# A convolution and a Laplace layer on one Trainium2 core: sums for two places in one run of matmuls, and three tiles for the mixed rows

## Chip, cores and metric

The kernel runs on one core of a Trainium2 chip. The metric is the device time of one execution in microseconds (us); the time before is the median of three runs.

## The reference

The input x has 16 images of 16 channels, 256 by 256, in float32. Two layers follow each other. Each normalises its input over groups of two channels and adds its result to that input.

```python
x = x + _L0_conv_ref(_gn(x), L0_conv_weight)          # a 3x3 circular convolution
x = x + _L1_conv_ref(_gn(x), ty, tx, pole1, pole2, residue)
```

The second layer is where the change lies:

```python
alpha = fft2(x)                                        # b i o x
A  = 1 / (omega1[:, None, None, None] - weights_pole1[None])
Bm = 1 / (omega2[:, None, None, None] - weights_pole2[None])
S  = einsum('ikpq,oikp,xikq->oxik', weights_residue, A, Bm)
output_residue1 = einsum('biox,oxik->bkox', alpha, S)  # mixing of channels, one matrix per frequency
x1 = ifft2(output_residue1).real
...
F  = einsum('kbpq,bipz->kbiqz', output_residue2, E1)
x2 = einsum('kbiqz,biqx->kizx', F, E2).real            # transient, with E1 = exp(pole1 ty), E2 = exp(pole2 tx)
return x1 + x2 / Nx / Ny
```

## The kernel before, in words

The work goes in four stages.

1. Convolution (to about 596 us): for each image, 3x3 convolution by small matmuls (L305). Results go to DRAM tensors `vD`. Tables for the second layer are made beside it.
2. Transform (to about 1190 us): channel by channel, folds on VectorE (DVE) and GpSimd (POOL), matmuls along y (L777, L785) and along x (L820). The spectra go to the DRAM tensor `aD`.
3. Mixing (to about 1866 us): for every frequency the 16 input channels are combined into 16 output channels. Spectra are read from `aD`, mixed rows are written to `yD`. This is the stage of the change.
4. Inverse transform, transient and output (to the end), L1325 to L1399.

**The mixing stage.** It runs over 32 groups g of four frequency rows, with four places n in each (L1222 to L1242). The instructions stand in each engine's queue in the order in which the loop writes them. At a place the loop does this:

- `sums(n, w_now)` (L1025): 16 matmuls, 32 on the hardware, on 64x32 tiles of the array, for the matrices S of the *next* group. They fill two PSUM banks; the pool of these banks, `p_s`, has four.
- `spread` (L1043): copies the two banks into the tile `sg` of the next group. For each bank, ScalarE (ACT) makes one copy (L1049) and DVE one shuffle (L1052).
- `mix` four times (L1111): 8 matmuls each, 16 on the hardware, of `sg` with the spectra `abd`, on 128x64 tiles, into a bank of the pool `p_mix`, which has four.
- Four copies from these banks into a tile `yt` (L1233): the first three on ACT and the last on DVE, or two and two when ACT has exponentials to do (`late`). The pool of `yt` has two buffers.
- Four stores of `yt` to `yD` (`store`, L1134), 128 KB each, and loads of the next group's spectra `abd` (`load`): at place 1 four of 256 KB (L1102), two before and two after the stores; at places 2 and 3 four of 128 KB each after the stores (L1107). The tiles `abd` have one buffer each, so a load follows the mixing that reads it. All of these are issued by SyncE (SP), in order.
- One step of `weights(g + 2)` on DVE (L903 to L919), at the third place the weight tile `w` on POOL (L930), and one step of `make_exps` (L1161 to L1214), which makes the tables of E1 and E2 on POOL and ACT.

Before the loop, `first_sums` (L1054) makes the first group's matrices and `finish_projections` (L1085) multiplies with the constant `jmat`. In the last group there are no sums; the first frequency is corrected by `unmix_first` (L1139), which loads four pieces from `yD` and stores them again.

Pools lie in SBUF one above the other. A tile that takes the memory of an earlier one waits for the last user of that one.

Of the kernel before, what the change touches and what calls it, by code (L numbers as in the profile page):

```python
# [9 lines left out]
FP = mybir.dt.float32  # L10
AF = mybir.ActivationFunctionType
ALU = mybir.AluOpType
# [4 lines left out]
B = 16  # L17
C = 16
N = 256
P = 128  # L20
PI = float(np.pi)
# [3 lines left out]
def conv_then_laplace_kernel(ctx: ExitStack, tc: tile.TileContext, a: dict, out: bass.AP):  # L25
# [15 lines left out]
    nc = tc.nc  # L41
    x = a["x"]

    cp = ctx.enter_context(tc.tile_pool(name="const", bufs=1))
# [6 lines left out]

    later_loads = []

    def const(name, shape):
        t = cp.tile(shape, FP, name=name, tag=name)
        later_loads.append((t, a[name]))
        return t

    cols = const("cols", [P, 24])
    kmask = const("kmask", [P, C])  # L60
    fold2 = const("fold2", [P, 2, 64])
    o2 = cp.tile([P, B, 2, 16], FP, name="o2", tag="o2")
    proj = cp.tile([P, 2, B, 16, 2], FP, name="proj", tag="proj")
    jmat = cp.tile([P, 3, P], FP, name="jmat", tag="jmat")

    def pitched(name, rows, row, *split):

# [27 lines left out]

    ptab = ExitStack()
    tp = ptab.enter_context(tc.tile_pool(name="tables", bufs=1))
    vmr = tp.tile([P, 2, B, C], FP, name="vmr", tag="vmr")


# [54 lines left out]
    own = m16[:, 0:C:2]  # L155
    load_consts()
    halves[1] = [load_x(1, h) for h in range(2)]
    nc.sync.dma_start(out=jmat, in_=a["jmat"])
    ones = tp.tile([P, P], FP, name="ones", tag="ones")
    nc.vector.memset(ones, 1.0)  # L160
    tiny = wp.tile([P, 8], FP, name="tiny", tag="tiny")
# [524 lines left out]
    for g in range(24 * B + 3):  # L686
# [4 lines left out]
        b, n = divmod(g, 24)  # L691
# [27 lines left out]
    def pool(stage, name, bufs=1, **kw):  # L719
        return stage.enter_context(tc.tile_pool(name=name, bufs=bufs, reuse_waits="tile", **kw))  # L720
# [11 lines left out]
    u0 = pool(p1, "u0")  # L732
# [162 lines left out]
    def weights(g):  # L895

        shape = [P, 32, 4]
        u = up["u" if g else "u0"].tile([P, 4, 32, 4], FP, name="u", tag="u")  # L900
        w, den, e, f = (u[:, j] for j in range(4))
        pr2, pre, pim = (prU[:, j].unsqueeze(2).to_broadcast(shape) for j in range(3))
        nc.vector.tensor_tensor(  # L903
            w,
            omg[:, g].unsqueeze(1).to_broadcast(shape),
            pims.unsqueeze(2).to_broadcast(shape),
            ALU.subtract,
        )
        nc.vector.tensor_tensor(den, w, w, ALU.mult)
        nc.vector.tensor_tensor(den, den, pr2, ALU.add)  # L910
        yield
        nc.vector.reciprocal(den, den)

        nc.vector.scalar_tensor_tensor(e, w, m1, pre, ALU.mult, ALU.add)
        nc.vector.scalar_tensor_tensor(f, w, nm0, pim, ALU.mult, ALU.add)
        yield
        v = up["v"].tile([P, 32, 2, 4], FP, name="v", tag="v")
        nc.vector.tensor_tensor(v[:, :, 0], e, den, ALU.mult)
        nc.vector.tensor_tensor(v[:, :, 1], f, den, ALU.mult)  # L919
        if g == 0:  # L920
            yield
        wt = wp.tile([P, 4, 8, 32], FP, name="w", tag="w")
        v2 = v.rearrange("p a r s -> p a (r s)")
        w4 = wt.rearrange("p a k (i m) -> p (a k) i m", i=4)
        if g == 0:
            for i in range(4):
                nc.scalar.activation(w4[:, :, i], v2, AF.Copy, scale=m4[:, i : i + 1])
            return wt
        full = [P, 32, 4, 8]
        nc.gpsimd.tensor_tensor(  # L930
            w4,
            v2.unsqueeze(2).to_broadcast(full),
            m4.unsqueeze(1).unsqueeze(3).to_broadcast(full),
            ALU.mult,
        )
        return wt
# [44 lines left out]
    ptab.close()  # L981


    yp = pool(p2, "yt", 2)
    g0 = pool(p2, "sg0")
    a0 = pool(p2, "abd0")
    wp = pool(p2, "w", 2)
    ep = pool(p2, "exps")
    up["u"] = pool(p2, "u")
    a1 = pool(p2, "abd2")  # L990
    zp = pool(p2, "between")
    tp = pool(p2, "ct")
    a2 = pool(p2, "abd3")
    g1 = pool(p2, "sg1")
# [10 lines left out]
        z.tile([P, 4, 4, 16, B], FP, name=f"abd{j}", tag=f"abd{j}") for j, z in ((2, a1), (3, a2))  # L1005
    ]

    zp.tile([P, 384], FP, name="between", tag="between")
    ct = tp.tile([P, 4, 8, N], FP, name="ct", tag="ct")
    nc.sync.dma_start(out=ct, in_=cD)  # L1010
    def next_step(steps, w):
# [42 lines left out]
    def first_sums():  # L1054
# [27 lines left out]
            load(0, jq)  # L1082
        return sg, w1

    def finish_projections():  # L1085


        for ro in range(2):
            ps = pm.tile([P, B, 16], FP, name="ps_o", tag="ps_mix")
            nc.tensor.matmul(ps, lhsT=jmat[:, 0], rhs=accs[:, ro], start=True, stop=False)  # L1090
            nc.tensor.matmul(ps, lhsT=jmat[:, 2 - ro], rhs=accs[:, 1 - ro], start=False, stop=True)
            nc.vector.tensor_copy(o2[:, :, ro], ps)

    def load(g, jq, rows=range(4)):

# [65 lines left out]
    def make_exps(which):  # L1161


        pl = ep.tile([P, C, 2], FP, name="s_pl", tag="s_pl")
        nc.sync.dma_start(out=pl, in_=a[f"pole_e{which + 1}"])
        t = ep.tile([P, N], FP, name="s_t", tag="s_t")
        nc.sync.dma_start(out=t, in_=a[("ty", "tx")[which]].to_broadcast([P, N]))
        sign, phase, turns = (cols[:, 2 + 3 * which + j : 3 + 3 * which + j] for j in range(3))
        pim = ep.tile([P, C], FP, name="s_pim", tag="s_pim")
        for _ in range(4):  # L1170
            yield
        nc.gpsimd.tensor_scalar(pim, pl[:, :, 1], sign, None, ALU.mult)
        for q in range(8):
            th = ep.tile([P, 2, N], FP, name="s_th", tag="s_th")
            rn = ep.tile([P, 2, N], FP, name="s_rn", tag="s_rn")
            tmp = ep.tile([P, 2, N], FP, name="s_tmp", tag="s_tmp")
            ex = ep.tile([P, 2, N], FP, name="s_ex", tag="s_ex")
            for j in range(2):
                i = 2 * q + j
                nc.gpsimd.tensor_scalar(th[:, j], t, pim[:, i : i + 1], None, ALU.mult)  # L1180
            nc.gpsimd.tensor_scalar(rn, th, 1.0 / (2 * PI), turns, ALU.mult, ALU.add)
            magic = 1.5 * 2.0**23
            nc.gpsimd.tensor_scalar(rn, rn, magic, None, ALU.add)
            nc.gpsimd.tensor_scalar(rn, rn, magic, None, ALU.subtract)
            yield
            c1 = 6.28125
            c2 = float(np.float32(1.93500518798828125e-3))
            c3 = 2 * np.pi - c1 - c2
            for c in (c1, c2, c3):
                nc.gpsimd.tensor_scalar(tmp, rn, float(c), None, ALU.mult)  # L1190
                nc.gpsimd.tensor_tensor(th, th, tmp, ALU.subtract)
                if c == c2:
                    yield
            nc.gpsimd.tensor_scalar(th, th, phase, 3.1415925, ALU.add, ALU.min)
            nc.gpsimd.tensor_scalar(th, th, -3.1415925, None, ALU.max)
            for j in range(2):
                i = 2 * q + j
                nc.scalar.activation(ex[:, j], t, AF.Exp, scale=pl[:, i, 0:1])
            yield True
            yield  # L1200
            nc.scalar.activation(th, th, AF.Sin)
            yield True
            nc.gpsimd.tensor_tensor(th, th, ex, ALU.mult)
            for op, eo in ((ALU.add, 0), (ALU.subtract, 1)):
                nc.gpsimd.tensor_tensor(
                    ex[:, :, eo * P : eo * P + P], th[:, :, 0:P], th[:, :, N - 1 : P - 1 : -1], op
                )
            yield
            for o in range(2 - which):
                nc.sync.dma_start(  # L1210
                    out=eD[which][o, :, 2 * q : 2 * q + 2].rearrange("p i e t -> p i (e t)"),
                    in_=ex,
                )
            yield  # L1214
# [1 line left out]
    p2.enter_context(tc.manual_schedule())  # L1216
    accs = yp.tile([P, 2, B, 16], FP, name="accs", tag="yt")
    ahead, wt = first_sums()
    finish_projections()
    unmix = None  # L1220
    exps, late = chain(make_exps(0), make_exps(1)), None
    for g in range(32):  # L1222
        sg, w_now = ahead, wt
        steps = weights(g + 2) if g < 30 else iter(())
        ahead = new_sg(g + 1) if g < 31 else None
        for n in range(4):
            evict = sums(n, w_now) if ahead is not None else []
            yt = yp.tile([P, 2, 4 * B, 16], FP, name="yt", tag="yt")
            if evict:
                spread(n, (ahead, [z.rearrange("p q n -> p n q") for z in evict]))  # L1230
            for m in range(4):
                o, src = mix(4 * n + m, sg, yt)
                (nc.vector.tensor_copy if m >= (2 if late else 3) else nc.scalar.copy)(o, src)  # L1233
            if n == 1 and g < 31:
                load(g + 1, n, (0, 1))
            store(g, n, yt)
            if g < 31:
                load(g + 1, n, (2, 3) if n == 1 else range(4))
            if n == 1 and unmix is not None:
                next(unmix, None)  # L1240
            wt = next_step(steps, None) or wt
            late = g and next(exps, None)  # L1242
        if g == 30:
            unmix = unmix_first()
            next(unmix)
# [364 lines left out]
```

## Time and profile before

| | |
|---|---|
| Median of three runs | 2617.32 us (2607.34 to 2626.05) |
| Profiled execution, its own time | 2623.94 us |
| Its span | 2622.1 us |
| PE busy, whole span | 2468.6 us (94%) |
| DVE / ACT / POOL busy | 1980.8 / 1432.6 / 1290.5 us |
| Granted TensorE clock | 0.986 |
| Mixing stage in the profile | about 1222 to 1866 us |
| Mixing matmuls (L1120), busy | 482.2 us, 8192 instructions |
| Copies into yt on ACT (L1233) | 184.1 us, 352 instructions of 592 ns |
| Idle time of ACT before these | 55.8 us, 42.2 of it until a store `yD<-yt` has landed |

Times are those of one profiled execution. "Busy" is the union of an engine's instructions; a wait is put down to the instruction or DMA that ended last before the waiting one began. PEld is the loading of weights into the array, which overlaps PE. SPq is SyncE's queue: all of its time is the issue of DMAs, and a wait for a semaphore is inside an instruction's duration.

### The profile page before, as it was taken

Reading aid. Unit: us, or ns where it says so; the run is one execution under the profiler, and the core shown is the slowest. Engines: PE = TensorE matmul, PEld = TensorE weight load, DVE = VectorE, ACT = ScalarE, POOL = GpSimd, SP = SyncE. Lnnn points to the kernel's source line nnn. Section 1 sums busy time; section 2 is a strip of 40 time slices with the busy share of each in tenths; the row PEclk is TensorE's granted clock in tenths of the full one; section 3 lists DMA queues with packets and bytes.
Section 4 is the critical chain, followed back from the end, with each engine's and each line's share of the span. In section 5 each row is a group of like instructions: output and inputs, shape, how many; then the busy total and the mean of one; then the engine's idle time right before and its main releaser. Section 6 shows DMA issues by size and latency. Waiting matters only on the chain.

```text
span 2622.1 us, 84262 instructions
## 1 busy us (share of the span) xinstructions
PE 2468.6 (94%) x35314; PEld 1885.3 (72%) x35314; DVE 1980.8 (76%) x3772; ACT 1432.6 (55%) x2599; POOL 1290.5 (49%) x1179
## 2 busy tenths in 40 slices
PE   5998999989999999998999999999799999999998
PEld 2444455567777777775878778788688888888887
DVE  7777788848888888887877878887276676667666
ACT  2565566666666666665666656666244444444443
POOL 1333378433333333333666645766555565555553
PEclk9999999989999999999999999999899999999999
DMA  7888878854655655655777777777988888888884
GB/s 274 276 279 282 294 270 294 297 211 177 240 195 209 242 220 194 245 225 190 225 229 214 226 225 222 222 227 228 253 302 289 291 292 279 299 289 287 291 287 174
DMA packets 318011, 653.17 MB, mean 249 GB/s; under 512 B 49174, under 2 KB 163990, under 8 KB 305728
## 3 DMA queue, kind: packets, MB, share of 16 engines
q1 hardware_dynamic: 316464, 640.57, 72.4%
q8 instruction: 278, 4.55, 0.7%
q0 software_dynamic: 896, 3.02, 0.4%
q10 hardware_dynamic: 272, 4.19, 0.4%
q14 instruction: 101, 0.83, 0.1%
HBM read 368.15 MB, written 280.36 MB: 247 GB/s over the span
## 4 chain that ended last, share of the span: by engine, by line
PE 58%; DVE 7%; DMA 4%; SPq 3%; ACT 3%; POOL 2%; issue 1%; ACTq 0%; DVEq 0%; POOLq 0%
PE ps_mix L1120 9%; PE ps_y L777 9%; PE ps_y L785 8%; PE ps_p L1361 7%; PE ps_f L1385 7%; PE ps_f L1386 7%; PE ps_x L820 5%; DMA yD<-yt 4%; PE ps_s L1032 2%; SPq L1134 2%; PE ps_h L1345 2%; PE psd L805 1%; DVE r L1394 1%; DVE ol L1396 1%; DVE ol L1397 1%
## 5 line engine op out<-in xcount | busy, mean ns | idle before, releaser
L1120 PE MATMUL ps_mix<-abd,sg 128*64 128x128 f32 x8192 | 482.2, 276 | 39.4 <-DMA yD<-yt 16.6
L1120 PEld LDWEIGHTS ps_mix<-abd,sg 128*64 128x64 f32 x8192 | 451.9, 138 | 92.9 <-ACT yt L1233 55.7
L1325 POOL TENSOR_TENSOR u<-yk 128x512 f32<-128x512 f32 (+1 forms) x268 | 358.2, 1369 | 314.7 <-PE ps_p L1361 249.1
L305 PE MATMUL ps_conv<-xt,wc 32*32 32x512 f32 x12288 | 445.6, 602 | 36.0 <-issue 26.1
L305 PEld LDWEIGHTS ps_conv<-xt,wc 32*32 32x32 f32 x12288 | 251.1, 103 | 217.6 <-issue 127.0
L793 ACT ACTIVATE t<-ps_y,vmr 128x384 f32<-128x384 f32 x512 | 297.1, 580 | 161.1 <-PE ps_y L785 161.1
L1052 DVE STREAM_SHUFFLE sg<-ps_s 128x512 f32<-128x512 f32 (+1 forms) x264 | 329.1, 1316 | 0.0
L777 PE MATMUL ps_y<-tabE,vq 128*128 128x256 f32 x1024 | 313.2, 388 | 11.0 <-DVE vq L766 9.4
L785 PE MATMUL ps_y<-tabO,vq 128*128 128x256 f32 x1024 | 305.9, 380 | 0.0
L275 POOL TENSOR_TENSOR pair<-pair,far 128x1024 f32<-128x1024 f32 x64 | 151.7, 2370 | 304.1 <-DVE pair L272 207.7
L1385 PE MATMUL ps_f<-pt,inv 128*128 128x256 f32 x1008 | 300.4, 380 | 0.0
L1386 PE MATMUL ps_f<-hs,ey 128*128 128x256 f32 x1008 | 299.8, 379 | 0.0
L1361 PEld LDWEIGHTS ps_p<-inv,u 128*128 128x128 f32 x2048 | 268.9, 193 | 35.4 <-POOL u L1329 10.9
L1389 DVE TENSOR_TENSOR r<-ps_f,q 128x256 f32<-128x256 f32 x256 | 107.0, 418 | 241.9 <-ACT q L1388 241.9
L1361 PE MATMUL ps_p<-inv,u 128*128 128x128 f32 x2048 | 276.2, 278 | 9.8 <-POOL u L1329 9.7
L1049 ACT ACTIVATE sg<-ps_s,mcol 128x512 f32<-128x512 f32 (+1 forms) x264 | 179.3, 689 | 192.2 <-DVE sg L1052 117.1
L777 PEld LDWEIGHTS ps_y<-tabE,vq 128*128 128x128 f32 x1024 | 189.6, 191 | 87.5 <-ACT q L833 51.2
L1388 ACT COPY q<-ps_f 128x256 f32<-128x256 f32 x256 | 95.4, 373 | 274.7 <-PE ps_f L1386 250.4
L1363 ACT COPY pt<-ps_p 128x512 f32<-128x512 f32 x256 | 151.5, 592 | 134.9 <-PE ps_p L1361 134.9
L765 POOL TENSOR_TENSOR vq<-vf 128x512 f32<-128x512 f32 x64 | 81.4, 1272 | 291.6 <-DVE vf L769 281.5
L785 PEld LDWEIGHTS ps_y<-tabO,vq 128*128 128x128 f32 x1024 | 195.4, 191 | 26.9
L1233 ACT COPY yt<-ps_mix 128x512 f32<-128x512 f32 x352 | 184.1, 592 | 55.8 <-DMA yD<-yt 42.2
(237 smaller groups left out, 3993.6 us busy)
## 6 DMA issues: line engine op xcount, KB each, us to landing
xt<-in_x SPq DMA_DIRECT2D x288, 258.0 KB
vD<-pair SPq DMA_DIRECT2D x256, 256.0 KB
yD<-yt SPq DMA_DIRECT2D x512, 128.0 KB
vl<-vD SPq DMA_DIRECT2D x128, 512.0 KB
out_y<-ol SPq DMA_DIRECT2D x128, 512.0 KB
s<-vD SPq DMA_DIRECT2D x126, 512.0 KB
aD<-spec SPq DMA_DIRECT2D x15, 4096.0 KB
yk<-yD SPq DMA_DIRECT2D x60, 1024.0 KB
```

The costliest lines, as they stand in the source:

```text
L305: nc.tensor.matmul(acc[r][32 * c : 32 * c + 32], lhsT=ready[b][0][rows, phase, tap], rhs=halves[b][u // 2][rows, q : q + 5 : 4, 2 - tap : ...
L777: nc.tensor.matmul(ps[:, 0:N], lhsT=vf[:, xo, 0, j], rhs=tabE[:, 0 : i + 2 : i + 1], start=True, stop=False, skip_group_check=True,)
L785: nc.tensor.matmul(ps[:, P : P + N], lhsT=vf[:, xo, 1, j], rhs=tabO[:, i : C + 1 : C - i], start=False, stop=True, skip_group_check=True,)
L793: nc.scalar.activation(t[:, xo, j].rearrange("p l n -> p (l n)"), ps[:, 0:384], AF.Copy, scale=vmr[:, 0, b0 + j, i : i + 1],)
L1049: nc.scalar.activation(to[..., k : k + 2], src[odd], AF.Copy, scale=nsgn)
L1052: nc.vector.stream_shuffle(to[..., C + k : C + k + 2], src[1 - odd], swap)
L1120: nc.tensor.matmul(ps[64 * t : 64 * t + 64, j], lhsT=sg[:, f : f + 2].rearrange("p f m -> p (f m)"), rhs=abd[jq][:, :, 2 * t + cc, 2 * jj ...
L1233: (nc.vector.tensor_copy if m >= (2 if late else 3) else nc.scalar.copy)(o, src)
L1325: nc.gpsimd.tensor_tensor(u[:, :, j].rearrange("p b (c n) -> p c b n", c=8), in0, in1, o)
L1361: nc.tensor.matmul(ps[:, at], lhsT=u[:, n], rhs=tab, start=True, stop=True)
L1385: nc.tensor.matmul(ps[:, e], lhsT=tab, rhs=pt[:, e], start=True, stop=False)
L1386: nc.tensor.matmul(ps[:, e], lhsT=ey[:, e], rhs=hs, start=False, stop=True)
```

## The change

- In the loop over places, the sums for places 0 and 1 are issued together before the mixing of place 0, and those for 2 and 3 before the mixing of place 2. `spread` stays at its place.
- The pool of `yt` gets a third buffer (8 KB a partition).
- The memory for it comes from elsewhere: `kmask` and `fold2` move to the pool of tables, which ends before the mixing; `o2` takes the memory of `proj`; `jmat` is loaded at the start of the mixing into the memory of a tile of `make_exps`; `weights` keeps `f` in the place of `w`; an empty tile ("between") goes; the rounding tiles of `make_exps` have half the size, so that its operations on two columns at once become operations on one, twice.

```diff
-    yp = pool(p2, "yt", 2)
+    yp = pool(p2, "yt", 3)
...
-    zp = pool(p2, "between")
...
-    zp.tile([P, 384], FP, name="between", tag="between")
...
-        u = up["u" if g else "u0"].tile([P, 4, 32, 4], FP, name="u", tag="u")
-        w, den, e, f = (u[:, j] for j in range(4))
+        u = up["u" if g else "u0"].tile([P, 3, 32, 4], FP, name="u", tag="u")
+        w, den, e = (u[:, j] for j in range(3))
...
-        nc.vector.scalar_tensor_tensor(f, w, nm0, pim, ALU.mult, ALU.add)
+        nc.vector.scalar_tensor_tensor(w, w, nm0, pim, ALU.mult, ALU.add)
...
+    jmat = ep.tile([P, 3, P], FP, name="jmat", tag="s_ex")
+    nc.sync.dma_start(out=jmat, in_=a["jmat"])
+
     def finish_projections():
+        o2 = cp.tile([P, B, 2, 16], FP, name="o2", tag="proj")
...
-            rn = ep.tile([P, 2, N], FP, name="s_rn", tag="s_rn")
-            tmp = ep.tile([P, 2, N], FP, name="s_tmp", tag="s_tmp")
+            rn = ep.tile([P, N], FP, name="s_rn", tag="s_rn")
+            tmp = ep.tile([P, N], FP, name="s_tmp", tag="s_tmp")
...
-            nc.gpsimd.tensor_scalar(rn, th, 1.0 / (2 * PI), turns, ALU.mult, ALU.add)
-            nc.gpsimd.tensor_scalar(rn, rn, magic, None, ALU.add)
-            nc.gpsimd.tensor_scalar(rn, rn, magic, None, ALU.subtract)
-            yield
...
-            for c in (c1, c2, c3):
-                nc.gpsimd.tensor_scalar(tmp, rn, float(c), None, ALU.mult)
-                nc.gpsimd.tensor_tensor(th, th, tmp, ALU.subtract)
-                if c == c2:
-                    yield
+            for j in range(2):
+                z = th[:, j]
+                nc.gpsimd.tensor_scalar(rn, z, 1.0 / (2 * PI), turns, ALU.mult, ALU.add)
+                nc.gpsimd.tensor_scalar(rn, rn, magic, None, ALU.add)
+                nc.gpsimd.tensor_scalar(rn, rn, magic, None, ALU.subtract)
+                for c in (c1, c2, c3):
+                    nc.gpsimd.tensor_scalar(tmp, rn, float(c), None, ALU.mult)
+                    nc.gpsimd.tensor_tensor(z, z, tmp, ALU.subtract)
+                yield
...
         for n in range(4):
-            evict = sums(n, w_now) if ahead is not None else []
+            if ahead is not None and n % 2 == 0:
+                banks = [sums(n + j, w_now) for j in range(2)]
+            evict = banks[n % 2] if ahead is not None else []
             yt = yp.tile([P, 2, 4 * B, 16], FP, name="yt", tag="yt")
```

More of the change, by code (lines that the diff above doesn't have):

```diff
@@ L52, in conv_then_laplace_kernel, with const @@
     later_loads = []
-    def const(name, shape):
-        t = cp.tile(shape, FP, name=name, tag=name)
+    def const(name, shape, home=cp):
+        t = home.tile(shape, FP, name=name, tag=name)
         later_loads.append((t, a[name]))
@@ L59, in conv_then_laplace_kernel @@
     cols = const("cols", [P, 24])
-    kmask = const("kmask", [P, C])
-    fold2 = const("fold2", [P, 2, 64])
-    o2 = cp.tile([P, B, 2, 16], FP, name="o2", tag="o2")
     proj = cp.tile([P, 2, B, 16, 2], FP, name="proj", tag="proj")
-    jmat = cp.tile([P, 3, P], FP, name="jmat", tag="jmat")
     def pitched(name, rows, row, *split):
@@ L97, in conv_then_laplace_kernel @@
     tp = ptab.enter_context(tc.tile_pool(name="tables", bufs=1))
+    kmask = const("kmask", [P, C], tp)
+    fold2 = const("fold2", [P, 2, 64], tp)
     vmr = tp.tile([P, 2, B, C], FP, name="vmr", tag="vmr")
@@ L157, in conv_then_laplace_kernel @@
     halves[1] = [load_x(1, h) for h in range(2)]
-    nc.sync.dma_start(out=jmat, in_=a["jmat"])
     ones = tp.tile([P, P], FP, name="ones", tag="ones")
@@ L918, in weights @@
         nc.vector.tensor_tensor(v[:, :, 0], e, den, ALU.mult)
-        nc.vector.tensor_tensor(v[:, :, 1], f, den, ALU.mult)
+        nc.vector.tensor_tensor(v[:, :, 1], w, den, ALU.mult)
         if g == 0:
@@ L1092, in finish_projections @@
             nc.vector.tensor_copy(o2[:, :, ro], ps)
+        return o2
     def load(g, jq, rows=range(4)):
@@ L1218, in conv_then_laplace_kernel @@
     ahead, wt = first_sums()
-    finish_projections()
+    o2 = finish_projections()
     unmix = None
```

## The prediction

> **What bounds the kernel now.** The profiled execution took 2623.94 us, its span is 2622.1 us. I read the page first, then the mixing stage alone: the table by windows, the waits, and SyncE's timeline and waits, since the chain of waits on the page names SPq and a DMA beside TensorE.
>
> The window of the mixing stage (columns: window, its length, busy us and count of PE, PEld, DVE, ACT, POOL, then clock, DMA share, GB/s):
>
> ```profile
> 1222.00:1866.00 644.00, 604.02 (x12164) 512.99 (x12160) 502.15 (x898) 407.45 (x682) 386.24 (x297) 0.98 0.77 224
> ```
>
> PE is busy 94% of it, and nothing else is near. That number misleads. In an undisturbed place the mixing matmuls start at 1504.60 and those of the next place at 1509.27: 4.67 us (mix 3.65, sums 1.02). Four places are a group, so 18.68 us. From the first store of mixed rows (1226.84) to the first store of the last group (1847.19) are 31 groups in 620.35 us, 20.01 us each. So PE loses 1.33 us a group, 41 us in all, and about 10 more in the last group, whose third place starts 11.9 us before its fourth. Who is late is in the waits from 1220 to 1866 us (who waits <- for whom: us in total, times, longest):
>
> ```profile
> ACT yt L1233 <- DMA yD<-yt: 42.2, 28, 10.3
> ...
> DVE yt L1233 <- DMA yD<-yt: 17.0, 12, 3.5
> PE ps_mix L1120 <- DMA yD<-yt: 16.6, 12, 3.2
> ```
>
> The copies into yt wait until the store of two places earlier has landed. That is what a third yt tile removes. But why do the stores land late? SyncE's timeline over one group (start, us, instructions in the row):
>
> ```profile
> 1479.43 3.18 SPq L1107 DMA_DIRECT2D abd<-aD  x4
> 1482.72 2.01 SPq L1134 DMA_DIRECT2D yD<-yt  x4
> 1484.84 4.25 SPq L1107 DMA_DIRECT2D abd<-aD  x4
> 1489.21 1.96 SPq L1134 DMA_DIRECT2D yD<-yt  x4
> 1491.27 1.24 SPq L1102 DMA_DIRECT2D abd<-aD  x2
> 1492.62 3.04 SPq L1134 DMA_DIRECT2D yD<-yt  x4
> 1495.70 1.24 SPq L1102 DMA_DIRECT2D abd<-aD  x2
> 1497.05 2.01 SPq L1134 DMA_DIRECT2D yD<-yt  x4
> 1499.16 0.58 SPq L1107 DMA_DIRECT2D abd<-aD  x1
> ```
>
> Between the rows lies 0.1 us: 18.93 of 19.73 us are issue. The first place's copies ended at 1484.48, its store was issued at 1489.21, behind four loads. So the queue of SyncE is full, and the yt wait is its shadow. SyncE's own waits say how much of its time is waiting for engines (counted from the end of the instruction before):
>
> ```profile
> SPq L1134 <- ACT yt L1233: 15.5, 28, 1.6
> SPq L1134 <- ACT sg L1049: 14.6, 32, 1.2
> ...
> SPq L1102 <- PE ps_mix L1120: 8.1, 11, 2.1
> SPq L1107 <- PE ps_mix L1120: 7.5, 17, 1.6
> SPq L1134 <- DVE yt L1233: 6.0, 4, 3.7
> ```
>
> With the smaller entries about 59 us. Issue goes on inside these figures; adding up, instruction by instruction, only the part beyond the usual duration (medians 448 ns for a store, 603 for a load), I get 27 us in the 620. This 27 us is all that SyncE can give back.
>
> **The rest of SyncE's time.** Undisturbed rows are 1.97 for four stores, 2.52 for four loads, 1.24 for two: 4 x 1.97 + 2 x 2.52 + 2 x 1.24 + eight gaps of 0.1 = 16.2 us a group, 16.7 with a store of exponentials. Observed 20.01; engines 27/31 = 0.9; the remaining 2.4 are issues that are stretched without waiting for a semaphore (such as the 3.04 and 4.25 above). The DMA view counts 96 instruction fetches of 16 KB in the window, and of the issues stretched by over 0.25 us three quarters overlap one, of the others one in twelve. The number of instructions stays, so I take this stretch to stay.
>
> **What the Trainium skill says.** "TensorEngine Tiling (Array Packing)", section Key Properties: changing the tiling mode drains the array. The trace agrees: 0.17 us idle before each run of sums (64x32 tiles), PEld idle 0.41 us before each run of mixing (128x64). "DMA: Bandwidth & Descriptors", section Anatomy of one DMA: about 2 us fixed, mostly the receipt of the last write; here the last store takes 5.91 us to land. The same page, section Issuing engines are not separate DMA queues, calls the time to initiate a DMA usually small beside the DMA; in this stage it differs, since issue fills the queue. "Runtime: NRT & Kernel Launch", section Instruction fetch mechanics: instructions come in 16 KiB blocks by DMA, mostly hidden; the packets are there, the hiding is not what SyncE's issues show.
>
> **The change, part by part.**
> *Third yt tile.* A copy waits for the store of three places earlier, 4.7 us more slack. The yD waits of ACT and DVE go. What is late next: PE runs ahead of SyncE until it waits for abd loads. The load of abd01 is issued around the store of place 1 and needed two places later; the other two are needed three places later. SyncE's queue stays full, so its pace is the bound: 20.01 - 0.87 = 19.13 us a group at best. Groups differ (without engine waits 17.3 to 22.7), the buffers level only part of it, and SyncE waits for PE in its short groups. I keep two thirds: 18 of 27 us. The other end is 0; the upper end 27.
> *Last group.* The copy of the third place no longer waits for the first's store, but the fourth's does, and the queue holds 8 stores, 4 for the first frequency and 8 stores: 5.6 + 2.5 + 4 = 12.1 us against 14.1. Gain 2 us.
> *Two places' sums in one run.* Two runs back to back took 1.96 us where one takes 1.09, so the second costs 0.87 instead of 1.02; mixing after mixing starts after 3.52 (last group) instead of 3.65. A pair is 1.02 + 0.87 + 3.52 + 3.65 = 9.06 against 9.34 us: 0.28 x 62 pairs = 17 us of PE. It is covered by SyncE's 9.57 a pair, so worth 0 now; if that cover goes, 17.
> *The four sum banks are now refilled together.* The second run waits for the shuffles of the last odd place. On DVE: mix of the even place ends at 1.89 + 3.52 = 5.41, result 0.25 later, copy 0.69, weights up to 1.30, two shuffles 2.52: 10.17. The bank is wanted at 9.06 + 0.87 = 9.93. So 0.2 us in the pairs with the long weights step, some 6 us in all, inside SyncE's 0.5 us a pair of slack: 0. DVE's load, 5.04 + 1.38 + 1.39 + at most 1.38 = 9.2 us in pairs with all extra copies, 8.4 on average, fits.
> *Exponentials in halves.* POOL gets nine more instructions in each of 16 passes. Half-size rows aren't in the trace for all forms; 128x256 against 128x512 for tensor_tensor is 730 to 1284 ns, 0.57. The split part is 0.70 + 2 x 1.49 + 3 x 2.77 = 12.0 us a pass, so 14% more is 1.7 us, 27 in all (0 if halves cost half; 192 if they cost the same). POOL is idle 258 of 644 us, 177.7 of them waiting for the weights' v: 0. If that cover were gone, the weights w behind it would hold the sums.
> *Moves.* The jmat load goes from the head to between ct and the first abd loads; SyncE is free from 1173.9 to 1209.2 there, and PE uses it after 1215: 0. The three small mixing constants load in the convolution stage instead of the second: three issues of about 0.35 us, hidden. o2 in proj's place waits for a sum that ends at 1203. The last yt tile lies under the first vl tile; vl's load stands behind a yk load that needs the same store: 0. f in w's place saves memory, not time.
>
> Sum: 18 + 2 = 20 us. Profiled 2624 - 20 = 2604; the median of the runs, 2617.3, is 6.6 below the profiled one, so 2597.
>
> **Rivals.**
> *PE becomes the bound* (0.20). If the stretched issues shrink once stores no longer bunch behind stalls, SyncE needs 16.7 us and PE 18.1 a group: 41 + 17 + 2 = 60 us, 2557. For it: 16.7 < 18.1. Against: the overlap with instruction fetches.
> *The wait only moves* (0.13): PE waits for abd what it waited for yt, and SyncE's 27 us of waiting stays. About 2613. For it: abd already ends waits (5.5 us at 1272, 5.95 at 1792 in the chain).
> *Four banks make it slower* (0.14). A copy into yt at the head of DVE's or ACT's queue, a table load (1.28 us) or the exponentials hold the shuffles of the odd place; before, two other banks covered that, now PE stands. A pair takes 9.06 + 0.1 + x; above SyncE's 9.57 it costs, above 10.0 it loses to today, and 1% slower needs x = 1.3. With x = 1.5: 0.66 x 62 = 41 us, 2658. Against: the walk above leaves x near 0.2.
>
> **How the numbers follow.** SyncE's pace: 0.53, its own range 2588 to 2607 (gain 10 to 29). A measurement of this kernel can tell about 1% from no change (its three runs lie 0.7% apart); 1% faster is 2591. A third of the likeliest case lies below it: 0.17 + 0.20 = 0.37 faster; 0.36 + 0.13 = 0.49 same; 0.14 slower. The range leaves out the lower half of the PE case and most of the slower one: 2563 to 2630.
>
> **What would show it.** Right: the yD waits of ACT and DVE fall below 15 us; PE's waits for abd loads rise; SyncE's rows stay 0.1 us apart; groups take 19.1 to 19.7 us; undisturbed pairs of places take about 9.06 us. Wrong: groups near 18.1 us with pauses in SyncE's timeline (PE bound), or PE waiting for sg shuffles before sums (banks).

## The result, and the profile after

The changed kernel takes 2641.84 us (median of 7 runs, 2633.85 to 2657.97), the kernel before 2617.32 (7 runs, 2607.34 to 2628.12). The ratio is 1.0099, with a 95% interval of 1.0079 to 1.0118: about 1% slower. 2597 was forecast, and the range ended at 2630. The profiled execution took 2639.36 us, its span is 2637.6.

The window of the mixing stage of the changed kernel, in the columns of the one shown before:

```profile
1222.00:1866.00 644.00, 593.51 (x11980) 517.27 (x11976) 489.88 (x885) 399.79 (x671) 412.36 (x438) 0.97 0.74 218
```

GpSimd is busy 412 us instead of 386, and the DMA share has gone down from 0.77 to 0.74. TensorE is busy 10 us less, but 184 fewer of its matmuls lie in this window. From the first store (1223.12) to the first of the last group (1861.45) 31 groups take 638.33 us, 20.59 us each instead of 20.01. What follows lasts 776 us in the changed kernel and 775 in the one before. So the loss is in the loop over groups, not at its ends. The window of exactly these 31 groups in the changed kernel:

```profile
1223.12:1861.45 638.33, 590.06 (x11922) 514.06 (x11920) 488.76 (x883) 399.53 (x671) 411.81 (x437) 0.97 0.74 218
```

Before, TensorE was busy 588.42 of 620.35 us there with as many matmuls, at a granted clock of 0.99. The pairs were to make it busy less, and it isn't.

The chain that ended last, as shares of the span by engine, on the changed kernel's page:

```profile
PE 56%; POOL 9%; DVE 7%; DMA 2%; issue 1%; SPq 1%; ACT 1%; DVEq 0%; ACTq 0%; POOLq 0%
```

And on the page of the kernel before:

```profile
PE 58%; DVE 7%; DMA 4%; SPq 3%; ACT 3%; POOL 2%; issue 1%; ACTq 0%; DVEq 0%; POOLq 0%
```

Before, SyncE's queue and the DMAs held 7% of it and GpSimd 2%; now they hold 3% and GpSimd 9%. An engine that sat idle for 258 of 644 us now holds a larger share of the chain than any but TensorE. The waits of the changed kernel from 1220 to 1878 us (who waits <- for whom: us in total, times, longest) say where:

```profile
PEld ps_s L1027 <- POOL w L927: 39.0, 15, 4.1
PE ps_s L1027 <- POOL w L927: 34.9, 10, 3.9
...
PE ps_mix L1120 <- DMA yD<-yt: 6.8, 6, 2.2
...
ACT yt L1235 <- DMA yD<-yt: 4.0, 4, 1.4
```

The yt wait is gone, 42.2 us to 4.0 on ScalarE and 17.0 to nothing on VectorE. In its place TensorE waits for w, the weights of the next group's sums: 39.0 us (the kernel before: 0.9). (The two rows for w show the same pauses, once at the loading of weights and once at the matmuls behind it; they overlap and aren't added.) TensorE's loss has moved from late stores to late weights. GpSimd's timeline about one such wait (start, us, instructions in the row, idle before):

```profile
1395.21 1.28 POOL L1203 TENSOR_TENSOR s_th<-s_th,s_ex 128x512 f32<-128x512 f32 x1
...
1398.11 1.83 POOL L1180 TENSOR_SCALAR s_th<-s_t,s_pim 128x256 f32<-128x256 f32 x2
...
1407.77 0.48 POOL L1187 TENSOR_SCALAR s_rn<-s_th,cols 128x256 f32<-128x256 f32 x1
...
1414.66 0.73 POOL L1192 TENSOR_TENSOR s_th<-s_th,s_tmp 128x256 f32<-128x256 f32 x1
1415.35 1.89 POOL L927 TENSOR_TENSOR w<-v,mcol 128x1024 f32<-128x1024 f32 x1
```

And before, about the same pass:

```profile
1400.53 1.83 POOL L1180 TENSOR_SCALAR s_th<-s_t,s_pim 128x256 f32<-128x256 f32 x2
...
1414.38 1.89 POOL L930 TENSOR_TENSOR w<-v,mcol 128x1024 f32<-128x1024 f32 x1 [2.15 <-DVE v L919]
```

From 1395 to 1415 the changed kernel's queue never stops, and w starts without idle time before it: it stood behind two steps of exponentials, 9.6 us (1398.11 to 1407.7) and 7.6 us (to 1415.3). Before, the two steps took 11.7 us, and GpSimd then stood 2.15 us until v came. In the changed kernel w ends at 1417.24; the mixing of that group's fourth place started at 1410.33, that of the next group's first, behind the two runs of sums that need w, at 1420.34, 10.01 us later, where 5.48 is the undisturbed value. The sums in between, and the window from 1418 to 1421 us:

```profile
1417.30 3.10 PE L1027 MATMUL ps_s<-ct,w 64*32 64x256 f32 x64 [3.26 <-POOL w L927]
...
1418.00:1421.00 3.00, 3.00 (x54) 1.73 (x40) 2.21 (x4) 1.42 (x2) 2.74 (x2) 0.50 0.74 216
```

So w costs more than the pause. After 3.26 us of standing, the two runs of sums take 3.10 us instead of 1.96, at a granted clock of 0.50: the throttle lets TensorE run at half its speed. The clock's records show ten such spells at 0.50 in the loop, of 3.4 or 6.8 us each, and two in the kernel before. Each of the ten begins close to the end of a pause of TensorE of 2.2 to 3.9 us; one pause of 3.6 us (at 1498 us) has none.

The groups by form in the window of the mixing give the costs (busy us, mean ns of one, idle before). Two of the five operations that are cut, in the kernel before:

```profile
L1190 POOL TENSOR_SCALAR s_tmp<-s_rn 128x512 f32<-128x512 f32 x48 | 71.6, 1491 | 4.1
L1191 POOL TENSOR_TENSOR s_th<-s_th,s_tmp 128x512 f32<-128x512 f32 x48 | 61.5, 1281 | 4.0
```

The same operations in the changed kernel, where each is two:

```profile
L1191 POOL TENSOR_SCALAR s_tmp<-s_rn 128x256 f32<-128x256 f32 x96 | 81.8, 852 | 8.2
L1192 POOL TENSOR_TENSOR s_th<-s_th,s_tmp 128x256 f32<-128x256 f32 x96 | 71.2, 741 | 8.0
```

One of these two operations on one column costs 0.57 to 0.58 of what it costs on two, and the gap of 0.08 us behind each instruction comes twice as often. With the other three (59.1 us before, 70.5 after) the passes grow by 31 us of work and 12 us of gaps, where 27 us of work and no gaps were forecast. That is more, but the size was not the main mistake. What had not been worked out is how a pass is cut into steps, one step a place. Before, the three steps last about 5.8, 5.8 and 6.5 us; now 9.6, 7.6 and 3.6, since the first two take whole columns. Two steps in a row hold 17.2 us instead of 11.7, in two places that last 9.0.

### The profile page after: what moved, and what is told of

Read it like the earlier page. It is cut to its first block, busy times and chain, and to the rows that moved or that the text cites. A ratio compares the mean times of both kernels' runs of the same rounds, so it can differ in the third digit from the quotient of the medians.

```text
span 2637.6 us, 84312 instructions
## 1 busy us (share of the span) xinstructions
PE 2471.5 (94%) x35314; PEld 1904.6 (72%) x35314; DVE 1975.6 (75%) x3772; ACT 1432.0 (54%) x2599; POOL 1324.2 (50%) x1323
## 4 chain that ended last, share of the span: by engine, by line
PE 56%; POOL 9%; DVE 7%; DMA 2%; issue 1%; SPq 1%; ACT 1%; DVEq 0%; ACTq 0%; POOLq 0%
PE ps_y L774 9%; PE ps_y L782 8%; PE ps_p L1363 7%; PE ps_mix L1120 7%; PE ps_f L1387 7%; PE ps_f L1388 7%; PE ps_x L817 5%; PE ps_s L1027 3%; POOL s_tmp L1191 2%; POOL s_th L1192 2%; PE ps_h L1347 2%; DMA yD<-yt 2%; PE psd L802 1%; POOL w L927 1%; DVE r L1396 1%
## 5 line engine op out<-in xcount | busy, mean ns | idle before, releaser
L1120 PE MATMUL ps_mix<-abd,sg 128*64 128x128 f32 x8192 | 472.5, 276 | 17.5 <-DVE yt L1235 7.3
L1388 PEld LDWEIGHTS ps_f<-hs,ey 128*128 128x128 f32 x1008 | 191.6, 190 | 26.0
```

The lines of the kernel that those rows point to most:

```text
L1120: nc.tensor.matmul(ps[64 * t : 64 * t + 64, j], lhsT=sg[:, f : f + 2].rearrange("p f m -> p (f m)"), rhs=abd[jq][:, :, 2 * t + cc, 2 * jj ...
L1388: nc.tensor.matmul(ps[:, e], lhsT=ey[:, e], rhs=hs, start=False, stop=True)
```

## The experiments

Theory: the halves make w late, and SyncE's queue is what paces the loop in any case. Rivals: the four sum banks refilled together cost the time; the third tile only moves waits; SyncE's fullness is no bound. The ratios are to the kernel before, with 95% intervals.

**The halves undone, at another price.** The operations on two columns are back, and tmp takes the memory of ex:

```diff
-            rn = ep.tile([P, N], FP, name="s_rn", tag="s_rn")
-            tmp = ep.tile([P, N], FP, name="s_tmp", tag="s_tmp")
-            ex = ep.tile([P, 2, N], FP, name="s_ex", tag="s_ex")
+            rn = ep.tile([P, 2, N], FP, name="s_rn", tag="s_rn")
+            tmp = ep.tile([P, 2, N], FP, name="s_tmp", tag="s_ex")
```

> The changed kernel with the exponentials' rounding steps on both columns at once again, as before the change (the tile tmp lies in ex's memory instead). Late w (theory): PE's 35 to 39 us of waits for w (L927) at the start of a group go, and with them the loss; what the third tile and the pairs are worth shows, 2590 to 2605 us. Four banks (rival 1): the loss comes from the shuffles that free the banks, so it stays near 2640. SyncE's pace (rival 2): the groups are already limited by issues, so taking away the wait for w moves it little, 2625 to 2640.

Measured: 2695.09 us, ratio 1.0286 [1.0260, 1.0313]. Slower still, and no test of the theory, for the shared memory brought a wait of its own (waits of this kernel in the mixing):

```profile
ACT s_ex L1198 <- POOL s_th L1190: 84.0, 15, 8.4
...
PEld ps_s L1027 <- ACT sg L1044: 43.2, 8, 6.7
```

ex can't be written before tmp is used up. The exponential stands at the head of ScalarE's queue, the sg copies behind it, and TensorE's sums wait for those.

**The kernel before with the halves alone.** Rounding tiles and loop over columns as in the change, nothing else.

> The kernel before with only the exponentials in halves. Late w: slower than before, but by less than in the changed kernel, since without pairs the last place of a group lasts 1.1 us longer and w has that much more time: 2622 to 2635 us. Four banks or SyncE's pace: as before, 2617.

Measured: 2641.21 us, 1.0072 [1.0050, 1.0095]. The loss is there with two yt tiles and without pairs. Its waits:

```profile
ACT yt L1233 <- DMA yD<-yt: 42.3, 29, 10.4
...
PEld ps_s L1032 <- POOL w L930: 22.5, 10, 3.1
```

The yt wait is the old one to a tenth, and 22.5 us of waiting for w have come. One caution: in the profiled execution the loop grows by only 4 us of the span's 12, and the rest stands before its first store. It is one of three executions of seven that took 2630 to 2637 us, at a mean granted clock of 0.985; the other four took 2641 to 2646, at 0.981. So the medians carry the verdict, not this one trace.

**The steps cut otherwise.** In the changed kernel the steps end after the second product of the first column and the first of the other:

```diff
-                yield
+                    if c == (c2, c1)[j]:
+                        yield
```

> The changed kernel with the same halves, but the step ends (yields) moved so that a place gets about 7, 5.5 and 7 us of POOL work instead of 9.5, 7.6 and 3.5. If w is late because of the two long steps ahead of it in POOL's queue: most of the loss goes, 2600 to 2615 us. If it is POOL's whole work that is too much: 2630 to 2642. Four banks: 2640.

Measured: 2634.92 us, 1.0056 [1.0035, 1.0076], with 28.4 us of waiting for w instead of 39.0. So where the steps end matters, but a more even cut brings back only some two fifths of the loss (1.0099 to 1.0056).

**The kernel before with the pairs alone.**

```diff
-            evict = sums(n, w_now) if ahead is not None else []
+            if ahead is not None and n % 2 == 0:
+                banks = [sums(n + j, w_now) for j in range(2)]
+            evict = banks[n % 2] if ahead is not None else []
```

> The kernel before with only the sums of two places in one run. Late w: POOL's work is as before, so little loss, and SyncE's queue hides the gain on PE: 2608 to 2618 us. Four banks: the loss of the change is here, 2635 to 2645 us.

Measured: 2620.42 us, 0.9993 [0.9979, 1.0007]. The pairs cost nothing and bring nothing. TensorE's weight loads wait 11.6 us for shuffles into sg, at no cost in time.

**Third tile and pairs with whole exponentials.** tmp goes into the unused half of proj's memory, beside o2:

```diff
-        o2 = cp.tile([P, B, 2, 16], FP, name="o2", tag="proj")
+        both = cp.tile([P, 2, B * 32], FP, name="o2", tag="proj")
+        o2 = both[:, 0].rearrange("p (b r m) -> p b r m", b=B, r=2)
...
+            tmp = spare
```

Here spare is both[:, 1]; the products are on two columns at once again.

> The changed kernel with the exponentials' rounding steps on both columns at once, as before the change; tmp now lies in the unused half of proj's memory, so that nothing waits for ex to be stored (which spoilt e1_full). Late w (theory): the 35 to 39 us of waits for w fall to a few, and third tile and pairs show their worth: 2590 to 2605 us. SyncE's pace alone (rival): the group takes as long whoever waits, 2615 to 2635.

> As f1_full_spare, but the sums place by place as before the change, so the third yt tile alone. SyncE's pace (theory for what is left): the pairs add nothing, so the same as f1_full_spare within 6 us, about 2597. If PE sets the pace: 12 to 17 us slower than f1_full_spare.

Measured: f1 2621.89 us, 1.0005 [0.9990, 1.0021]; f2, the same without the pairs, 2623.80 us, 1.0008 [0.9992, 1.0023]. Without the halves the changed kernel is the kernel before, to 0.2%. The waits of f1:

```profile
PE ps_mix L1121 <- DMA yD<-yt: 22.1, 15, 4.5
...
ACT yt L1236 <- DMA yD<-yt: 11.3, 7, 4.2
...
PEld ps_s L1027 <- POOL w L927: 6.8, 9, 1.7
```

Most of the wait for w is gone. So is most of the copies' wait for stores, 59 us of it before and 20 now, and yet no time was won: groups last 19.97 us (before 20.01). SyncE's own account, an estimate added up from its trace as in the prediction, shows why. Without the time beyond usual that it waits for engines it needs 19.17 us a group (before 19.13), and it still waits 0.80 us (before 0.88). The third tile left that waiting almost where it was.

f1 differs from the changed kernel only in the exponentials and the place of tmp, so its 31 groups show what the halves cost TensorE:

```profile
1224.20:1843.40 619.20, 578.74 (x11904) 510.89 (x11902) 490.32 (x883) 398.03 (x671) 380.66 (x293) 0.99 0.76 225
```

The changed kernel's loop is 19.1 us longer. TensorE stands idle for 7.8 us of that and is busy 11.3 us longer, with practically the same matmuls. The spells at half clock (ten, in f1 three) fit the second part; that the pauses bring them was not tried.

**Loads on ScalarE's queue.** The loads of the pair of quarters (abd01) issued on ScalarE, in f1 (f3) and in the kernel before (f4):

```diff
-                nc.sync.dma_start(
+                (nc.scalar if g else nc.sync).dma_start(
```

> As f1_full_spare, with the four loads of abd01 per group (L1102) issued by ACT instead of SyncE. SyncE's pace: its work falls by 2.5 us a group and PE becomes the bound, 2560 to 2580 us. If SyncE's queue isn't the bound: as f1_full_spare, or slower by ACT's time for the issues (2600 to 2620).

> The kernel before with these loads issued by ACT, two yt tiles. SyncE's pace: stores are issued earlier, the waits of ACT and DVE for yD (59 us) fall by more than half, 2580 to 2595 us. If the two tiles are what costs, whatever SyncE does: 2610 to 2625.

Measured: 2733.74 us, 1.0433 [1.0404, 1.0462], and 2697.28 us, 1.0297 [1.0268, 1.0326]. Both are slower than any case expected, and no test of SyncE. ScalarE's timeline in f4:

```profile
1503.99 2.62 ACTq L1102 DMA_DIRECT2D abd<-aD  x4
1506.65 1.52 ACT L1049 ACTIVATE sg<-ps_s,mcol 128x512 f32<-128x512 f32 x2 [2.83 <-PE ps_mix L1120]
```

The sg copies come behind 2.6 us of issue, and ScalarE's work is what TensorE waits for now (PEld for yt of ScalarE: 101.9 us, before 55.7). That this explains the whole loss was not tried.

**Fewer issues on SyncE.** The fourth quarter's loads are left out after the first group, in f1 and in the kernel before:

```diff
-        if jq == 0:
+        if jq == 0 or (jq == 3 and g):
```

> The changed kernel with full-size exponentials (their products in the spare half of o2's memory, 2621.9 us), without the loads of the fourth quarter of the spectra after the first group: SyncE issues 4 of its 28 transfers a group less, so from the second group on that quarter is mixed from the first group's spectra (this part of the computation is left out). Its 12 kernels so far all show SyncE needing 19.1 to 19.3 us a group for issuing, and groups of 19.9 to 20.0 us. If SyncE's queue is the pace: the four issues last 0.60 us and more each, 2.5 us a group, so the group falls towards TensorE's own 18.1 us: -1.6 to -2.0 us by 31 groups, 2560 to 2573 us. If SyncE's fullness is only a coincidence and the waits are TensorE's with the memory (bandwidth), the 0.5 MB less in some 4.5 MB a group would give at most a third of that: 2605 to 2618. If something else is the pace: 2617 to 2626.

> The kernel before without the loads of the fourth quarter of the spectra after the first group (4 of SyncE's 28 issues a group; that quarter is mixed from the first group's spectra, so this part of the computation is left out). The changed kernel with full-size exponentials and without these loads took 2584.7 us, 37 us less than with them. If SyncE's queue was the pace and the two yt tiles cost nothing beside it, this one falls as far, 2580 to 2590 us (TensorE's own 18.7 us a group would give 2577 to 2585). If the two tiles and the unpaired sums are a second limit right behind SyncE, it falls less, 2592 to 2612, and the difference to 2584.7 is what the third tile and the pairs are worth once SyncE has room. If SyncE is not the pace for this kernel: 2614 to 2624.

> The changed kernel with full-size exponentials and without the fourth quarter's loads after the first group (that quarter is mixed from the first group's spectra, so this part of the computation is left out) once more, 2584.7 us before, for its profile. If SyncE is no longer the pace, TensorE is busy over 97% of the loop and the group lasts 18.1 us at its full clock; since the time says some 18.8, either TensorE is granted a lower clock than in the kernel before without these loads (1.00 there, in the loop), or it still waits, for SyncE's loads of the other quarters or for evictions: then 0.5 us and more a group stand in the waits.

Measured: g1 2584.67 us, 0.9865 [0.9843, 0.9887], without a profile; j1 2584.68 us, 0.9858 [0.9831, 0.9885]; k1, which is g1 again, 2587.81 us, 0.9895 [0.9872, 0.9919], with a profile. Four of 28 issues fewer are worth 35 us in the kernel before. TensorE paces it then: this is j1's window inside the loop.

```profile
1230.00:1810.00 580.00, 576.78 (x11828) 489.47 (x11826) 485.94 (x881) 394.95 (x663) 379.54 (x288) 1.00 0.73 210
```

TensorE is busy 99.4%; place after place takes the undisturbed 4.67 us; the mean group is 18.79 us against the 18.68 of the prediction. The copies' waits for stores are down to 11.8 and 9.4 us with two yt tiles: these waits were the shadow of SyncE's queue, and a third tile had little of its own to remove. The loads that are left out take their bytes with them, so this run alone does not tell issues from memory traffic.

By the prediction TensorE has 0.6 us a group less to do in k1, but its group is no shorter (18.82 us). Its waits, 1220 to 1810 us:

```profile
PEld ps_mix L1121 <- ACT yt L1236: 15.5, 38, 0.6
...
PEld ps_s L1027 <- POOL w L927: 13.5, 12, 1.7
...
PE ps_s L1027 <- POOL w L927: 10.4, 9, 1.5
```

TensorE's matmuls wait 10.4 us for w here, and 1.6 in j1. In k1 the sums of the first two places both stand at the group's start, where w is the last to come. Over the 31 groups TensorE is busy 9.6 us less than in j1 (569.8 against 579.4), not the 17 us of the prediction, and idle 10.3 us more (13.5 against 3.2). So what the pairs save is lost again, 8.8 us of it to w. Why they save 9.6 and not 17 is open.

**More issues on SyncE.** f1 with two transfers of 64 bytes ahead of each store:

```diff
+        for h in range(2):
+            nc.sync.dma_start(out=xD[4 * g + jq : 4 * g + jq + 1, h], in_=cols[0:1, 0:16])
```

> The changed kernel with full-size exponentials (2621.9 us), with two more transfers of 64 bytes ahead of each place's store, from a constant tile to memory that nothing reads: 248 more issues on SyncE in the mixing loop, and no bytes to speak of. If SyncE's queue is the pace, each costs its issue: [...]25 to 110 us, so 2645 to 2735 us. If SyncE is not the pace, or has slack of about 1 us a group as its engine waits show, the first 1 us a group is hidden: 2620 to 2630 at 0.1 us each.

Measured: 2682.77 us, 1.0230 [1.0202, 1.0257], some 60 us over f1. SyncE's timeline:

```profile
1502.46 0.74 SPq L1136 DMA_DIRECT2D xD<-cols  x2
1503.31 1.76 SPq L1138 DMA_DIRECT2D yD<-yt  x4
1505.17 3.24 SPq L1109 DMA_DIRECT2D abd<-aD  x4
```

The small issues last 0.34 us in the mean, 2.7 us a group. SyncE's need goes from 19.17 to 21.93 us, and its waiting for engines from 0.80 to 0.14: the first 0.66 us came out of the waiting, the other 2.1 us are the 22.07 - 19.97 by which the group grew. 248 transfers with next to no bytes cost some 60 us, so issues alone, without memory traffic, make this loop longer. Whether traffic has a part in the 35 us of j1 as well, this run doesn't tell.

**w on another engine.** The changed kernel with halves and all, and w on VectorE:

```diff
-        nc.gpsimd.tensor_tensor(
+        nc.vector.tensor_tensor(
             w4,
```

> The changed kernel as it is (exponentials in halves, 2641.8 us), with the product w of the weights on VectorE and not on GpSimd. If the loss of the change is that w stands in GpSimd's queue behind the longer halves, and the next group's first sums wait for w, the waits for w (74 us in the changed kernel's profile) go, and the time is that of the kernel with full-size exponentials: 2617 to 2628 us, a little more if VectorE's own 1 to 2 us a group delays evictions. If the halves hurt in another way (GpSimd's traffic, the exponentials that ScalarE has in its in-order queue, the time of VectorE's steps), it stays at 2635 to 2648.

Measured: 2625.51 us (14 runs), 1.0017 [0.9998, 1.0035]. The halves are as many as in the changed kernel and no shorter (911 and 755 ns in the mean, there 852 and 741), and most of its loss is gone (1.0099 to 1.0017) once w doesn't stand behind them. So it is through w that the halves reach TensorE. In place of w the weight loads wait for shuffles of VectorE, most of it behind running matmuls, which wait 15.6 us themselves (the 74 us for w in the expectation add the two overlapping rows; it is 39.0):

```profile
PEld ps_s L1027 <- DVE sg L1047: 37.0, 52, 1.5
```

**A version that beats both.** The fourth quarter's loads move to GpSimd's queue at the first place of the group that uses them, and w to VectorE; nothing is left out. k2 is the kernel before with this, k3 is f1 with it:

```diff
-                nc.sync.dma_start(
+                (nc.gpsimd if g and jq == 3 else nc.sync).dma_start(
                     out=abd[jq][s::4, s]
...
-            if g < 31:
+            if g < 31 and n < 3:
                 load(g + 1, n, (2, 3) if n == 1 else range(4))
+            if g and n == 0:
+                load(g, 3)
```

> The kernel before with nothing left out, but with the fourth quarter's four loads a group issued on GpSimd at the first place of the group that uses them, and w on VectorE. SyncE has 24 issues a group as in the kernel before without these loads (2584.7 us); GpSimd has 4 x 0.55 us a group more and 1.9 us of w less, in a queue with over 200 us of idle time. If SyncE's issues are the pace and nothing else: 2580 to 2592 us. If the same bytes, moved from another queue, bring back part of it (memory bandwidth): 2592 to 2608. If GpSimd's queue stands on the loads' wait for TensorE and the exponentials come late behind it, as on ScalarE's queue: 2615 us and more.

> The same two moves in the changed kernel with full-size exponentials (third tile and pairs kept, nothing left out). Beside the kernel before with these moves: equal within 3 us if the pairs and the third tile are worth nothing even with room on SyncE, as the two kernels without the loads were (2584.7 both); 8 to 18 us faster if TensorE's 0.6 us a group shows now: 2565 to 2580. With GpSimd's queue as a new wait: 2615 us and more.

Measured: k2 2597.57 us, 0.9931 [0.9915, 0.9946]; k3 2604.82 us, 0.9958 [0.9944, 0.9973]. Half of what leaving the loads out gave is to be had by moving them, with w moved as well; what each move gives alone was not tried. The time lies in the range that was named beforehand for memory traffic as part of the limit, and no run here separates that from other causes. Groups last 19.14 us in k2, and TensorE needs 18.7; its matmuls wait 10.1 us for copies of ScalarE into yt. Why those are late (VectorE has w as well, GpSimd's exponentials wait behind the loads) is open. k3 seems 7 us slower than k2, though their intervals touch, and its waits name the rival of the four banks (the matmuls themselves wait 9.2 us for the shuffles):

```profile
PEld ps_s L1027 <- DVE sg L1047: 30.7, 54, 1.3
```

## Why the prediction was wrong

- **What bounds the kernel: right, and shown.** SyncE's queue paces the loop (j2 with more issues; j1, g1 with fewer issues and fewer bytes), and the yt wait is its shadow (j1).
- **Exponentials in halves: this step failed.** It set 1.7 us a pass against GpSimd's 258 us of idle time and put down 0. Measured, as differences of ratios: 0.72% (e2), 0.82% (the changed kernel against j3) and 0.94% (against f1), so 19 to 25 us of 2617. The idle time is an average over the stage, most of it ended by v's arrival. At the places where exponentials run the queue is full, and w stands in it with a due time, the start of the next group. The prediction named this ("If that cover were gone, the weights w behind it would hold the sums") and gave it no price and no case among the rivals. Seeing it needed only the pass cut into its steps: 17.2 us in the first two instead of 11.7, where GpSimd stood 2.15 us before w. The spells at half clock were in no term of the prediction either. All seven executions of the changed kernel were granted 0.977 to 0.982 of the clock in the mean, those with w on VectorE (j3) 0.982 to 0.988.
- **Third tile, 18 us, and last group, 2 us: failed in size.** f2 has the third tile alone, with the moves that pay for it: 1.0008 [0.9992, 1.0023], at most 2 us of gain. The yD waits of ScalarE and VectorE did fall below 15 us each, as foretold, but SyncE's waiting for engines stayed, at 0.80 us a group in f1. The prediction took two thirds of it as won, though it said itself that SyncE waits for TensorE in its short groups. What follows the last group's first store lasts 774.90 us before and 774.95 in f2. The rival "the wait only moves", which gave 2613, was right that SyncE's waiting stays. Its other half, that TensorE then waits for loads instead, hardly shows: the mixing matmuls wait 22.3 us for DMAs in f1, 19.4 before. What keeps the 0.80 us there was not tried.
- **Pairs: right for this kernel.** 3.54 + 5.48 = 9.02 us undisturbed, against 9.06, and worth 0 (e4, f1 against f2). With the cover gone they are still worth 0, not 17 (k1 against j1): TensorE is busy 9.6 us less, and waits for w take back most of that.
- **Four banks: right that they cost nothing now** (e4). TensorE's waits for shuffles show once VectorE has more to do (k3).
- **Moves: right within what one trace shows.** The first store comes at 1223.12 instead of 1226.84; a gain of a few us, if any.
- **PE becomes the bound: didn't happen,** for the stretched issues stayed (SyncE's need 19.13 before, 19.17 in f1).

Summed up: 20 us of gain were forecast and none came; 0 of loss, and about 1% came.

## What to carry to other kernels

Idle time of an engine is no cover for work that goes ahead of an instruction with a due time: cut the added work into the pieces in which the program issues it, and lay them beside the instruction that others wait for. A pause of TensorE can cost more than its length: look at the granted clock behind it. When a queue of DMA issues is full, the waits at its buffers can be its shadow; here another buffer removed the waits and no time, and fewer issues on that queue brought the time. A buffer that is paid for with memory from elsewhere is priced with the code that gave the memory up.

## What the runs showed of the hardware

- A transfer of 64 bytes holds SyncE's queue for 0.34 us in the mean, one of 128 KB for 0.50 (stores) or 0.71 us (loads), all in j2: with next to no bytes an issue still costs two thirds of a store's. The Trainium skill, "DMA: Bandwidth & Descriptors", section Issuing engines are not separate DMA queues, takes the time to initiate a DMA as usually small relative to the DMA. Nothing here speaks against that for a single one; but 28 issues a group, one behind the other, fill 19 of 20 us of SyncE's queue, so in this loop it is their sum that binds.
- On GpSimd an operation on 128x256 costs 852 or 741 ns where one on 128x512 costs 1491 or 1281, and each instruction some 0.08 us more between it and the next.
- In the changed kernel's loop the granted clock stood at 0.50 in ten spells of 3.4 or 6.8 us, each beginning within 1.5 us of the end of a pause of TensorE of 2.2 to 3.9 us. In the spell of 1418 us a matmul of the sums took 627 ns instead of 376. A pause of 3.6 us without a spell shows that length alone does not decide; the rule was not sought.
- The product w (128x1024) takes 1.23 us on VectorE (j3) and 1.89 on GpSimd.
